# V of three batches by seven block products instead of eight, in an attention stage that shares its block sums

## The chip, the cores and the metric

The kernel runs on one core of a Trainium2 chip. Its time is the device time of one execution in microseconds. The core's engines are called PE (matrix products), ACT, DVE and POOL (elementwise work) and SP (which issues most DMAs); each works through its own queue in order, and they wait for each other through semaphores.

## What is computed

A decoder layer on x of 4 batches, 1024 tokens, 512 features, all in float32: self-attention, a gated convolution with a second input and a feed-forward product, each followed by a residual addition and a normalisation. The change touches only the attention's projections:

```python
q = _lin(_lin(x, wq_w, wq_b), vq_w, vq_b)      # k and v likewise
q = q.reshape(b, s, hc, H).transpose(2, 0, 1, 3)   # 32 heads of width 16
scores = jnp.einsum('cbqh,cbkh->cbqk', q, k) / scale
attn = jax.nn.softmax(scores, axis=-1)
o = jnp.einsum('cbqk,cbkh->cbqh', attn, v)
```

The two linear maps of each projection are folded into one 512x512 matrix (w_q, w_k, w_v) at the start.

## The kernel before

**Units and steps.** The attention works on 32 units, u = 0 to 31: batch b = u // 8 and a group g = u % 8 of four heads. A unit has 32 steps, h = 0 to 31, in an order written out by hand (the loop from line 754). Each step issues two things on PE: `nat` (L568), raw scores of unit u+1, of which DVE takes the row maxima (`mx`, L584), and `scores` (`st`, L638) of unit u, of which ACT takes the exponential (`at`, L649). After every second step comes one slot of other PE work: at h % 4 == 1 a weighing (`av`, L664: the weights times V, then a copy on ACT, L675, or an addition on DVE, L677), at h % 4 == 3 one piece of the list `fill`. At steps 15 and 31 DVE joins the maxima of half a unit (`neg`, L590) and transposes them, and SP moves them into the rows of q.

**What fills the slots.** In units 0 to 23 a unit's eight slots hold six pieces of the q or k projection of later units and two pieces of V of the next batch. All of these use `by_quarters` (L59), whose four matmuls of 32 columns of weights each go to the four quarters of PE. A V piece (`project_v`, L531 to 542) is 16 matmuls of 256 columns: 128 tokens by half the features, over all four 128-rows of the input. DVE adds the bias while it writes the piece from PSUM into `v_sb` (L536), whose rows have 17 words per head. Units 24 to 31 hold no V.

**q and k by seven products.** From unit 4 on, q and k use Strassen-Winograd block products: the 512 x 1024 x^T is cut into 2x2 blocks (b11, b21, b12, b22), two neighbouring 128-column blocks of the weights are cut into a11 to a22, and `product` (L451 to 493) computes one of the seven products in parts of 256 or 512 columns, 8 matmuls each. ACT copies each part out of PSUM (L477, L479), into its place in a pack or into one of two `rooms`; POOL adds the parts together (L482 to L493). `sum_x` (L428) makes four sums of x^T's blocks with POOL once per batch, in 1024 columns each, and `sum_w` (L442) four sums of the weights' blocks. `to_quadrants` (L392) moves a finished pack to the units' q and k with DMAs.

**PSUM.** `st`, `av` and the pieces of `fill` share `ps_st`, four banks in rotation; `nat` has two tiles of two banks each.

**The end of a unit.** `normalise` (L683) runs in four stages at steps 5, 9, 13 and 20 of the next unit: SP fetches the denominators, DVE inverts them, SP spreads them by DMA over the tile `rbc` (L703; two tiles, used in turn), POOL multiplies (`o_n`, L711) and SP stores the result. At step 5 of unit 24, loads for the later stages begin, and POOL adds a bias to the loaded residual `y` (L100).

Of the kernel before, what the change touches and what calls it, by code (L numbers as in the profile page):

```python
# [8 lines left out]
F32 = mybir.dt.float32  # L9
AF = mybir.ActivationFunctionType  # L10
ALU = mybir.AluOpType
# [3 lines left out]
P = 128  # L15
B, S, D = 4, 1024, 512
NH, HD = 32, 16
# [3 lines left out]
VW = HD + 1  # L21
# [230 lines left out]
def attention(ctx, tc, a, attn_d, ident, shared, hand):  # L252
    nc = tc.nc
# [4 lines left out]
    w_v = shared.tile([P, FT, D], F32, tag="w_v", name="w_v")  # L258
# [7 lines left out]
    def load_x(b):  # L266
# [2 lines left out]
            nc.sync.dma_start(t[:, f, :], a["xT"][b, f * P : (f + 1) * P, :])  # L269
        return t  # L270


    once = ctx.enter_context(tc.tile_pool(name="aonce", bufs=1))


    v_sb = []
# [7 lines left out]
    nc.vector.tensor_reduce(  # L284
        ones_row, ident.rearrange("p (j r) -> p r j", j=4)[:, HD, :], AX.X, ALU.add
    )
    q_ts, k_ts, rbcs = [], [], []
    for n, pool in ((3, shared), (1, once)):
        t = pool.tile([P, 8 if n == 3 else 2, S], F32, tag=f"qk{n}", name=f"qk{n}")
        for i in range(n):  # L290
# [8 lines left out]
    extra = shared.tile([P, 4, FT, TR], F32, tag="xf", name="extra").rearrange("p e t m -> p (e t m)")  # L299
    packs.append(extra[:, 0 : 2 * S].rearrange("p (n s) -> p n s", n=2))  # L300
    rooms = [extra[:, n : n + 256] for n in (2 * S, 2 * S + 256)]
    x_sums = []
    for n in range(2):
        t = shared.tile([P, 4, D + 1], F32, tag="u", bufs=2, name=f"x_sums{n}")
        x_sums += [t[:, 0:2, 0:512], t[:, 2:4, 0:512]]
    w_sums = shared.tile([P, FT, D], F32, tag="w_f", name="w_sums")
    w_sums = w_sums.rearrange("p (n i) (k o) -> p n (i k) o", n=2, o=P).rearrange("p n (i k) o -> p n i k o", i=4)

# [4 lines left out]
        negs.append(t)  # L313

    rbcp = ctx.enter_context(tc.tile_pool(name="arbc", bufs=1))
    for i in range(2):
        t = rbcp.tile([P, S], F32, tag=f"rbc{i}", name=f"rbc{i}")
        nc.gpsimd.memset(t, 0.0)
        rbcs.append(t)

    small = ctx.enter_context(tc.tile_pool(name="asmall", bufs=2))
    dpool = ctx.enter_context(tc.tile_pool(name="rec_d", bufs=2, space=bass.MemoryType.DRAM))
# [6 lines left out]
    xts = {}  # L329
# [54 lines left out]
                nc.vector.tensor_copy(w_d[:, f, :], pts[f])  # L384
    units = [(b, g) for b in range(B) for g in range(NG)]
    NU = len(units)
    QW = 256
    HS = 32


# [34 lines left out]

    def sum_x(b):  # L428
        b11, b21, b12, b22 = (
            xts[b][:, 2 * k : 2 * k + 2, 512 * t : 512 * t + 512] for t in range(2) for k in range(2)  # L430
        )
        t1, t2, t3, t4 = x_sums
        for dst, one, two in ((t1, b12, b11), (t2, b22, t1), (t3, b22, b12), (t4, t2, b21)):
            nc.gpsimd.tensor_tensor(dst, one, two, ALU.subtract)

    def blocks_of_w(p, which):
        w = (w_q, w_k)[which]
        return [
            w[:, 2 * k : 2 * k + 2, gg * P : (gg + 1) * P] for gg in (p % 4, p % 4 + 1) for k in range(2)
        ]  # L440

    def sum_w(p, which):  # L442
        a11, a12, a21, a22 = blocks_of_w(p, which)
        s1, s2, s3, s4 = (w_sums[:, which, i, :, :] for i in range(4))
        tt = nc.gpsimd.tensor_tensor
        tt(s1, a21, a22, ALU.add)
        tt(s2, s1, a11, ALU.subtract)
        tt(s3, a11, a21, ALU.subtract)
        tt(s4, a12, s2, ALU.subtract)

    def product(p, which, i, t0, n):  # L451

        b, gg = divmod(p, 4)
        a11, a12, _, a22 = blocks_of_w(p, which)
        s1, s2, s3, s4 = (w_sums[:, which, k, :, :] for k in range(4))
        t1, t2, t3, t4 = x_sums
        b11, b21, _, b22 = (
            xts[b][:, 2 * k : 2 * k + 2, 512 * t : 512 * t + 512] for t in range(2) for k in range(2)
        )
        left, right = {  # L460
            1: (a11, b11), 2: (a12, b21), 3: (s4, b22), 4: (a22, t4), 5: (s1, t1), 6: (s2, t2), 7: (s3, t3)
        }[i]
        cols = slice(t0, t0 + n)
        pt = ps_st.tile([P, 512], F32, tag="st", name=f"part{i}_{p}_{which}_{t0}")[:, 0:n]
        by_quarters(nc, pt, lambda k: left[:, k, :], lambda k: right[:, k, cols], 2)
        c11, c12, c21, c22 = (
            packs[which][:, o, 512 * t + t0 : 512 * t + t0 + n] for o in range(2) for t in range(2)
        )
        if i in (2, 3, 4):
            dst = rooms[0]  # L470
            rooms.reverse()
            dst = dst[:, 0:n]
        else:
            dst = {1: c11, 5: c22, 6: c12, 7: c21}[i]
        if i in (1, 7):
            bias = (b_q, b_k)[which][:, gg : gg + 1] if i == 1 else b_diff[:, which, gg // 2 : gg // 2 + 1]
            nc.scalar.activation(dst, pt, AF.Identity, bias=bias, scale=1.0)  # L477
        else:
            nc.scalar.copy(dst, pt)  # L479
        add = nc.gpsimd.tensor_add  # L480
        if i == 6:
            add(c12, c12, c11)  # L482
        elif i == 2:
            add(c11, c11, dst)
        elif i == 7:
            add(c21, c21, c12)
        elif i == 5:
            add(c12, c12, c22)
            add(c22, c22, c21)
        elif i == 3:  # L490
            add(c12, c12, dst)
        elif i == 4:
            nc.gpsimd.tensor_sub(c21, c21, dst)  # L493
# [37 lines left out]
    def project_v(b, t, half):  # L531

        pt = ps_st.tile([P, QW], F32, tag="st", name=f"v{b}_{t}_{half}")
        cols = slice(half * QW, half * QW + QW)
        by_quarters(nc, pt, lambda f: xts[b][:, f, t * P : (t + 1) * P], lambda f: w_v[:, f, cols])
        nc.vector.tensor_add(  # L536
            v_sb[b % 2][:, t, 16 * half * VW : 16 * (half + 1) * VW].rearrange("p (c h) -> p c h", h=VW)[
                :, :, 0:HD
            ],
            pt.rearrange("p (c h) -> p c h", h=HD),  # L540
            b_v[:, cols].rearrange("p (c h) -> p c h", h=HD),
        )

    def v_pieces(b, t):
        return [lambda half=half: project_v(b, t, half) for half in range(2)]

    def out_piece(b, t, c0, c1):
        pt = ps_st.tile([P, QW], F32, tag="st", name=f"po{b}_{t}_{c0}")
# [133 lines left out]

    def normalise(u, stage):  # L683
        b, g = units[u]
        o_sb, rbc = o_sbs[u], rbcs[u % 2]
        if stage == 0:

            den = small.tile([P, 32], F32, tag="den", name=f"den{u}")
            for j in range(4):
                nc.sync.dma_start(  # L690
                    den[32 * j : 32 * j + 32, :],
                    o_sb[32 * j + HD : 32 * j + HD + 1, :].rearrange("p (q r) -> p q r", r=32),
                )
            recs[u] = den
        elif stage == 1:
            rec = small.tile([P, 32], F32, tag="rec", name=f"rec{u}")
            nc.vector.reciprocal(rec, recs[u])
            rec_d = dpool.tile([4, S], F32, tag="rec_d", name=f"rec_d{u}")
            nc.sync.dma_start(rec_d.rearrange("j (q r) -> (j q) r", r=32), rec)
            recs[u] = rec_d  # L700
        elif stage == 2:
            for j in range(4):
                nc.sync.dma_start(  # L703
                    rbc[32 * j : 32 * j + HD, :], recs[u][j, :].partition_broadcast(HD)
                )
        else:
            o_n = onp.tile([P, 2, 512], F32, tag="o_n", name=f"o_n{u}")
            for half in range(2):
                cols = slice(512 * half, 512 * half + 512)

                nc.gpsimd.tensor_mul(  # L711
                    o_n[:, :, half * 256 : half * 256 + 256],
                    o_sb[:, cols].rearrange("p (s e) -> p e s", e=2),
                    rbc[:, cols].rearrange("p (s e) -> p e s", e=2),
                )

            for j in range(4):
                c = 4 * g + j
                for e in range(2):
                    r = c // 2 * 32 + e * HD  # L720
                    nc.sync.dma_start(
                        attn_d[c % 2 * 2 + b // 2][r : r + HD, b % 2 * 512 : b % 2 * 512 + 512],
                        o_n[32 * j : 32 * j + HD, e, :],
                    )
# [20 lines left out]
        nc.vector.tensor_tensor(b_diff[:, which, :], bias[:, 1::2], bias[:, 0::2], ALU.subtract)  # L745
    for piece in early[2:] + qk_pieces(0, 1) + folds[:5]:
        piece()
    sum_x(0)
    sum_w(2, 0)
    sum_w(2, 1)  # L750
    nc.sync.dma_start(b_d.rearrange("(t p) -> p t", p=P), b_vc)
# [2 lines left out]
    for u in range(-1, NU):  # L754
# [13 lines left out]
        if u == -1:  # L768
            fill = folds[5:] + qk_pieces(1, 0) + qk_pieces(1, 1) + [
                piece for t in range(NT) for piece in v_pieces(0, t)  # L770
            ] + fill
        elif units[u][0] + 1 < B:
            vs = v_pieces(units[u][0] + 1, units[u][1])
            fill = fill + vs if w == 3 else vs + fill
        if w == 2 and p + 2 < NU // 2:
            due.setdefault((u, 24), []).append(lambda p=p: sum_w(p + 2, 0))
        if w == 0 and u >= 0 and p < NU // 2:
            due.setdefault((u, 24), []).append(lambda p=p: sum_w(p, 1))
        if w == 3 and p % 4 == 2 and p // 4 + 1 < B:
            due.setdefault((u, 28), []).append(lambda p=p: sum_x(p // 4 + 1))  # L780
        if u == -1:
            xts[1] = load_x(1)
        elif units[u][1] == 5 and units[u][0] + 2 < B:
# [37 lines left out]
        else:  # L821
# [38 lines left out]
                    hand.load_residual(2)  # L860
            assert not fill
        if u == -1:
            setup.close()
            atp = ctx.enter_context(tc.tile_pool(name="at", bufs=14))
            obuf = ctx.enter_context(tc.tile_pool(name="obuf", bufs=2))
            onp = ctx.enter_context(tc.tile_pool(name="onp", bufs=1))
# [332 lines left out]
```

## Time and profile before

| what | value |
|---|---|
| median of 3 runs | 2428.03 us (2427.80 to 2428.67) |
| the profiled execution | 2427.53 us |
| its span, first to last instruction | 2425.7 us |
| PE busy | 2410.5 us |
| DVE busy | 1747.9 us |
| ACT busy | 1329.0 us |
| POOL busy | 588.5 us |
| mean granted clock of PE | 0.999 |

The profile lists, for groups of instructions, the line, the engine, the operation, the tiles written and read, the count, the busy time, the mean time of one in ns, and the idle time before them with what ended it. Its timeline gives start, duration, engine, line and tiles of single instructions or runs of them, all from the start of the span; a bracket names the idle time before and the instruction that ended it. PEld is the loading of weights into PE, which overlaps its matmuls; each float32 matmul leaves two records. The chain is the work that ended last, followed back from the end. The stage of units 0 to 23 lies between about 149 and 1464 us.

### The profile page before, as it was taken

What the parts mean: (1) busy time and instruction counts of PE and PEld (TensorE: products, weight loads), DVE (VectorE), ACT (ScalarE), POOL (GpSimd) and SP (SyncE); (2) the same over time, 40 slices, a digit from 0 to 9 for tenths busy, and PEclk for the clock granted to TensorE, in tenths of its full rate; (3) what the DMA queues carried; (4) which work ended last, traced back from release to release, by engine and by line L of the source; (5) the groups of instructions that cost most, each with busy time, mean ns of one, the idle gap of its engine ahead of it and who ended that gap; (6) DMA issues with size and microseconds to landing.
All of it is one profiled execution on the core that took longest, in us unless ns stands there. A gap on an engine that the chain in (4) does not pass through costs nothing.

```text
span 2425.7 us, 70210 instructions
## 1 busy us (share of the span) xinstructions
PE 2410.5 (99%) x30380; PEld 1626.6 (67%) x30380; DVE 1747.9 (72%) x2197; ACT 1329.0 (55%) x2593; POOL 588.5 (24%) x537
## 2 busy tenths in 40 slices
PE   9999999999999999999999999999999999999998
PEld 5556666666666666666666666566666799747994
DVE  3577777777777777777777777677777477878677
ACT  1056666666666666666666666566666723411333
POOL 5011311111122212111311201311210267422661
PEclk9999999999999999999999999999999999999999
DMA  6200112011001111111110012102200242160311
GB/s 222 59 3 17 28 23 56 17 30 26 17 17 30 21 54 22 25 21 20 27 25 17 17 34 93 41 17 48 89 17 12 81 149 87 70 226 18 122 35 70
DMA packets 80838, 121.45 MB, mean 50 GB/s; under 512 B 39072, under 2 KB 39328, under 8 KB 80528
## 3 DMA queue, kind: packets, MB, share of 16 engines
q1 hardware_dynamic: 79808, 115.77, 16.8%
q8 instruction: 239, 3.92, 0.7%
q10 hardware_dynamic: 720, 1.18, 0.1%
q14 instruction: 71, 0.58, 0.1%
HBM read 80.77 MB, written 18.35 MB: 41 GB/s over the span
## 4 chain that ended last, share of the span: by engine, by line
PE 97%; DVE 1%; POOL 0%; ACT 0%; DMA 0%; issue 0%; SPq 0%; DVEq 0%; POOLq 0%; ACTq 0%
PE nat L568 22%; PE av L664 20%; PE st L638 18%; PE part L59 8%; PE pc L948 6%; PE pa L948 6%; PE v L59 5%; PE pf L1032 4%; PE po L59 2%; PE po L241 2%; PE proj L59 1%; PE fold L377 1%; PE fold L59 1%; PE tr L1024 0%; PE nats L568 0%; POOL y L100 0%
## 5 line engine op out<-in xcount | busy, mean ns | idle before, releaser
L584 DVE TENSOR_REDUCE mx<-nat 128x2 f32<-128x1024 f32 x1008 | 1188.0, 1220 | 402.8 <-PE st L638 375.0
L649 ACT ACTIVATE at<-st 128x512 f32<-128x512 f32 x2016 | 1043.2, 603 | 541.6 <-PE st L638 529.8
L568 PE MATMUL nat<-qk 32*128 32x512 f32 x4032 | 1011.8, 614 | 0.5 <-DVE mx L584 0.5
L638 PE MATMUL st<-qk 32*128 32x256 f32 x8064 | 1002.0, 387 | 3.7 <-ACT extra L479 3.7
L638 PEld LDWEIGHTS st<-qk 32*128 32x128 f32 x8064 | 685.7, 184 | 48.8 <-ACT extra L479 4.5
L664 PE MATMUL av<-at,v_sb 128*32 128x256 f32 x8192 | 499.6, 383 | 1.4 <-ACT at L649 1.4
L568 PEld LDWEIGHTS nat<-qk 32*128 32x128 f32 x4032 | 344.0, 184 | 220.1 <-DVE mx L584 136.6
L664 PEld LDWEIGHTS av<-at,v_sb 128*32 128x32 f32 x8192 | 241.7, 110 | 223.1 <-ACT at L649 90.2
L948 PE MATMUL pc<-xf,w 128*128 128x171 f32 x1024 | 159.9, 308 | 0.6 <-DVE o_sb L677 0.6
L948 PE MATMUL pa<-xf,w 128*128 128x171 f32 x1024 | 159.8, 308 | 0.0
L948 PEld LDWEIGHTS pc<-xf,w 128*128 128x128 f32 x1024 | 152.0, 189 | 1.7 <-DVE o_sb L677 1.1
L948 PEld LDWEIGHTS pa<-xf,w 128*128 128x128 f32 x1024 | 152.1, 189 | 0.0
L711 POOL TENSOR_TENSOR o_n<-o_sb,rbc 128x512 f32<-128x512 f32 x64 | 97.7, 1547 | 170.9 <-DMA rbc<-rec_d 132.8
L959 ACT ACTIVATE u<-u,b_c 128x512 f32<-128x512 f32 x64 | 46.2, 721 | 161.1 <-DVE u L958 161.1
L59 PE MATMUL v<-w_v,xT 128*32 128x256 f32 x2048 | 121.7, 382 | 0.0
L1032 PE MATMUL pf<-w_f,xq_t 128*128 128x512 f32 (+1 forms) x264 | 115.2, 581 | 1.7 <-ACT xq_t L1026 1.5
L677 DVE TENSOR_TENSOR o_sb<-av,o_sb 128x256 f32<-128x256 f32 x128 | 54.4, 425 | 73.6 <-PE av L664 73.1
L170 POOL TENSOR_TENSOR w<-w 128x512 f32<-128x512 f32 x64 | 81.8, 1311 | 92.9 <-DMA w<-in_conv_wT 61.1
L482 POOL TENSOR_TENSOR qk<-qk 128x256 f32<-128x256 f32 x14 | 10.1, 724 | 380.1 <-ACT qk L479 379.9
L59 PEld LDWEIGHTS v<-w_v,xT 128*32 128x32 f32 x2048 | 61.1, 109 | 55.0 <-ACT at L649 16.5
L675 ACT COPY o_sb<-av 128x256 f32<-128x256 f32 x128 | 48.0, 375 | 78.0 <-PE av L664 63.4
L59 PE MATMUL part<-x_sums,w_sums 128*32 128x256 f32 (+1 forms) x896 | 83.6, 490 | 0.0
(139 smaller groups left out, 1810.4 us busy)
## 6 DMA issues: line engine op xcount, KB each, us to landing
w<-in_conv_wT SPq DMA_DIRECT2D x32, 512.0 KB
u<-in_ctx SPq DMA_DIRECT2D x16, 1024.0 KB
xT<-in_xT SPq DMA_DIRECT2D x16, 512.0 KB
qk<-qk SPq DMA_DIRECT2D x128, 64.0 KB
qk<-extra SPq DMA_DIRECT2D x128, 64.0 KB
rbc<-rec_d SPq DMA_DIRECT2D x128, 64.0 KB
attn<-o_n SPq DMA_DIRECT2D x256, 32.0 KB
big<-attn SPq DMA_DIRECT2D x4, 2048.0 KB
```

The source lines that it names most:

```text
L59: nc.tensor.matmul(pt[r, :], lhsT(f)[:, r], rhs(f), start=f == 0, stop=f == tiles - 1)
L170: self.nc.gpsimd.tensor_tensor(w[:, i, tap, :], w[:, i, 0, :], w[:, i, 1, :], op)
L241: nc.tensor.matmul(pt, attn_t[:, f, t * P : (t + 1) * P], self.w_o[:, f, cols], start=f == 0, stop=f == FT - 1)
L568: nc.tensor.matmul(pts[n], q_ts[u % 4][r : r + 32, qt * P : (qt + 1) * P], k_ts[u % 4][r : r + 32, kh * 512 : kh * 512 + 512], start=True, ...
L584: nc.vector.tensor_reduce(mxs[u][:, qt, 2 * pair : 2 * pair + 2, kh], pt, AX.X, ALU.max, negate=True)
L638: nc.tensor.matmul(st[:, k * QW : k * QW + QW], k_ts[u % 4][r : r + 32, kt * P : (kt + 1) * P], q_ts[u % 4][r : r + 32, qq * QW : qq * QW ...
L649: nc.scalar.activation(at, st, AF.Exp, scale=0.25)
L664: nc.tensor.matmul(av[32 * j : 32 * j + 32, :], v_sb[b % 2][:, kt, c * VW : c * VW + 32], ats[u, 2 * i + n // 2, j][:, n % 2 * QW : n % 2 ...
L677: nc.vector.tensor_add(o, av, o)
L711: nc.gpsimd.tensor_mul(o_n[:, :, half * 256 : half * 256 + 256], o_sb[:, cols].rearrange("p (s e) -> p e s", e=2), rbc[:, cols].rearrange( ...
L948: nc.tensor.matmul(pt, w[:, i, tap, o : o + P], xf[:, tap, i, :], start=i == 0, stop=i == FT - 1)
L1032: nc.tensor.matmul(pt, xq_ts[b, t][:, f, :], hand.w_f[:, f, cols], start=f == 0, stop=f == FT - 1)
```

## The change

- **V of batches 1 to 3** is computed by the same seven block products. Two 256-column halves of w_v and two 256-row halves of its input make the weights' blocks; POOL forms their four sums once, at step 8 of unit 0. Tokens t and t + 4 (in tiles of 128) are the two token blocks, so a product for one t is 128 tokens by 256 columns over half the input: 8 matmuls. There are 28 of them per batch: 12 PSUM tiles take two, 4 tiles take one. ACT copies each product into a room, and POOL adds it to one, two or three places of `v_sb`, for product 1 with the bias: 52 additions of 256 columns per batch. Batch 0 keeps `project_v`.
- **x^T's sums** are shared by q, k and V. The third (b22 - b12) is written in place of b12, and the four subtractions are spread over steps 26, 28, 30 and 0 instead of standing together at step 28. The freed quarter of `x_sums` and a new tile hold w_v's sums.
- **Rooms**: four instead of two until unit 24 (the new pair is the tile of `b_o`, which is loaded in unit 24).
- **One `rbc` tile** instead of two.
- **Order**: in units with u % 4 == 1 or 3 (w = 0 and 2) the V pieces stand third and sixth of the eight slots instead of first and second; the other units keep their order.

```diff
-    for i in range(2):
-        t = rbcp.tile([P, S], F32, tag=f"rbc{i}", name=f"rbc{i}")
-        nc.gpsimd.memset(t, 0.0)
-        rbcs.append(t)
+    rbc = rbcp.tile([P, S], F32, tag="rbc", name="rbc")
+    nc.gpsimd.memset(rbc, 0.0)
...
+    t = shared.tile([P, D], F32, tag="b_o", name="rooms")
+    rooms += [t[:, 0:256], t[:, 256:512]]
...
+    def sums_of_x(b):
+        b11, b21, b12, b22 = blocks_of_x(b)
+        t1, t2, t4 = x_sums
+        sub = nc.gpsimd.tensor_sub
+        return [
+            lambda: sub(t1, b12, b11),
+            lambda: sub(t2, b22, t1),
+            lambda: sub(t4, t2, b21),
+            lambda: sub(b12, b22, b12),
+        ]
...
+    def v_products(b, parts):
+        pt = ps_st.tile([P, 512], F32, tag="st", name=f"v{b}_" + "_".join(f"{i}{t}" for i, t in parts))
+        made = []
+        for n, (i, t) in enumerate(parts):
+            left, right = operands(i, v_blocks, v_sums, b)
+            part = pt[:, n * QW : n * QW + QW]
+            by_quarters(nc, part, lambda k: right[:, k, t * P : t * P + P], lambda k: left[:, k, :], 2)
+            made.append(part)
...
+        kept = []
+        for part in made:
+            kept.append(room())
+            nc.scalar.copy(kept[-1], part)
...
+            if i == 1:
+                add(c12, x, b1)
+                add(c21, x, b2)
+                add(c22, x, b2)
+            elif i == 2:
+                add(c11, c12, x)
+            elif i == 4:
+                nc.gpsimd.tensor_sub(c21, c21, x)
+            else:
+                for c in {3: (c12,), 5: (c12, c22), 6: (c12, c21, c22), 7: (c21, c22)}[i]:
+                    add(c, c, x)
+
+    v_parts = [[(1, t), (2, t)] for t in range(4)] + [[(3, 0), (3, 1)], [(3, 2), (3, 3)]]
+    v_parts += [[(6 - n, t), (7 - 3 * n, t)] for t in range(3) for n in range(2)]
+    v_parts += [[(i, 3)] for i in (6, 7, 5, 4)]
...
-            vs = v_pieces(units[u][0] + 1, units[u][1])
-            fill = fill + vs if w == 3 else vs + fill
+            b, g = units[u][0] + 1, units[u][1]
+            v1, v2 = (lambda n=n, b=b: v_products(b, v_parts[n]) for n in (2 * g, 2 * g + 1))
+            fill = {
+                0: fill[:2] + [v1] + fill[2:4] + [v2] + fill[4:],
+                1: [v1, v2] + fill,
+                2: fill[:2] + [v1] + fill[2:4] + [v2] + fill[4:],
+                3: fill + [v1, v2],
+            }[w]
...
-            due.setdefault((u, 28), []).append(lambda p=p: sum_x(p // 4 + 1))
+            for when, work in zip(((u, 26), (u, 28), (u, 30), (u + 1, 0)), sums_of_x(p // 4 + 1)):
+                due.setdefault(when, []).append(work)
+        if u == 0:
+            due.setdefault((0, 8), []).append(lambda: sum_blocks(v_blocks, v_sums))
+        if u == 24:
+            del rooms[:]
+            rooms.extend(extra[:, n : n + 256] for n in (2 * S, 2 * S + 256))
```

More of the change, by code (lines that the diff above doesn't have):

```diff
@@ L270, in load_x @@
         return t
+    QW = 256
     once = ctx.enter_context(tc.tile_pool(name="aonce", bufs=1))
@@ L286, in attention @@
     )
-    q_ts, k_ts, rbcs = [], [], []
+    q_ts, k_ts = [], []
     for n, pool in ((3, shared), (1, once)):
@@ L305, in attention @@
         x_sums += [t[:, 0:2, 0:512], t[:, 2:4, 0:512]]
+    t = x_sums.pop()
+    v_sums = [t[:, i, :].rearrange("p (k o) -> p k o", k=2) for i in range(2)]
+    t = once.tile([P, 2, 2, QW], F32, tag="v_sums", name="v_sums")
+    v_sums += [t[:, i, :, :] for i in range(2)]
     w_sums = shared.tile([P, FT, D], F32, tag="w_f", name="w_sums")
@@ L386, in attention @@
     NU = len(units)
-    QW = 256
     HS = 32
@@ L418, in qk_pieces, with blocks_of_x @@
         ]
[L428 to L434, printed above, removed]
+    def blocks_of_x(b):
+        return [xts[b][:, 2 * k : 2 * k + 2, 512 * t : 512 * t + 512] for t in range(2) for k in range(2)]
+    def sums_of_x(b):
[8 more added lines that the diff above has]
+        ]
     def blocks_of_w(p, which):
@@ L442, in sum_w, with sum_blocks @@
     def sum_w(p, which):
-        a11, a12, a21, a22 = blocks_of_w(p, which)
-        s1, s2, s3, s4 = (w_sums[:, which, i, :, :] for i in range(4))
+        sum_blocks(blocks_of_w(p, which), [w_sums[:, which, i, :, :] for i in range(4)])
+    def sum_blocks(blocks, sums):
+        a11, a12, a21, a22 = blocks
+        s1, s2, s3, s4 = sums
         tt = nc.gpsimd.tensor_tensor
@@ L449, in sum_w, with operands, room @@
         tt(s4, a12, s2, ALU.subtract)
+    def operands(i, blocks, sums, b):
+        a11, a12, _, a22 = blocks
+        s1, s2, s3, s4 = sums
+        t1, t2, t4 = x_sums
+        b11, b21, t3, b22 = blocks_of_x(b)
+        return {
+            1: (a11, b11), 2: (a12, b21), 3: (s4, b22), 4: (a22, t4), 5: (s1, t1), 6: (s2, t2), 7: (s3, t3)
+        }[i]
+    def room():
+        rooms.append(rooms.pop(0))
+        return rooms[-1]
     def product(p, which, i, t0, n):
         b, gg = divmod(p, 4)
[L454 to L462, printed above, removed]
+        left, right = operands(i, blocks_of_w(p, which), [w_sums[:, which, k, :, :] for k in range(4)], b)
         cols = slice(t0, t0 + n)
@@ L469, in product @@
         if i in (2, 3, 4):
-            dst = rooms[0]
-            rooms.reverse()
-            dst = dst[:, 0:n]
+            dst = room()[:, 0:n]
         else:
@@ L545, in v_pieces @@
         return [lambda half=half: project_v(b, t, half) for half in range(2)]
+    v_blocks = [w_v[:, 2 * k : 2 * k + 2, QW * o : QW * o + QW] for o in range(2) for k in range(2)]
+    def v_products(b, parts):
[6 more added lines that the diff above has]
+            made.append(part)
+        heads = lambda x, w: x.rearrange("p (c h) -> p c h", h=w)[:, :, 0:HD]
+        b1, b2 = (heads(b_v[:, o * QW : o * QW + QW], HD) for o in range(2))
+        kept = []
+        for part in made:
+            kept.append(room())
+            nc.scalar.copy(kept[-1], part)
+        add = nc.gpsimd.tensor_add
+        for (i, t), x in zip(parts, kept):
+            c11, c12, c21, c22 = (
+                heads(v_sb[b % 2][:, tt, 16 * o * VW : 16 * (o + 1) * VW], VW) for o in range(2) for tt in (t, t + 4)
+            )
+            x = heads(x, HD)
+            if i == 1:
[12 more added lines that the diff above has]
+    v_parts += [[(i, 3)] for i in (6, 7, 5, 4)]
     def out_piece(b, t, c0, c1):
@@ L684, in normalise @@
         b, g = units[u]
-        o_sb, rbc = o_sbs[u], rbcs[u % 2]
+        o_sb = o_sbs[u]
         if stage == 0:
@@ L747, in attention @@
         piece()
-    sum_x(0)
+    late_sum = sums_of_x(0)
+    for work in late_sum[:3]:
+        work()
     sum_w(2, 0)
@@ L862, in attention @@
         if u == -1:
+            late_sum[3]()
             setup.close()
```

## The prediction

> **What bounds the kernel now.** I read the page first: its busy shares, its slices, the chain that ended last.
>
> ```profile
> PE 2410.5 (99%) x30380; PEld 1626.6 (67%) x30380; DVE 1747.9 (72%) x2197; ACT 1329.0 (55%) x2593; POOL 588.5 (24%) x537
> ...
> PE 97%; DVE 1%; POOL 0%; ACT 0%; DMA 0%; issue 0%; SPq 0%; DVEq 0%; POOLq 0%; ACTq 0%
> PE nat L568 22%; PE av L664 20%; PE st L638 18%; PE part L59 8%; PE pc L948 6%; PE pa L948 6%; PE v L59 5%; PE pf L1032 4%; PE po L59 2%; PE po L241 2%; PE proj L59 1%; PE fold L377 1%; PE fold L59 1%; PE tr L1024 0%; PE nats L568 0%; POOL y L100 0%
> ```
>
> PE is 97% of the chain and the V products (v, L59) are 5% of it. In the table by stages PE is busy 451.00 of 451 us from 149 to 600 us, and as fully up to 1464 us, while POOL is busy 79.10 of those 451. So in units 0 to 23, where all of the change lies, only PE's own work counts, until some other engine makes PE wait. The waits of PE agree: in the whole run one wait for an evacuation is above 2 us (PE st <- ACT extra L479, 3.7 us, once, in unit 24).
>
> Next, what a product costs **in its place**. PE runs a strict beat: two steps of scores and maxima (1.93 us), then one slot, filled in turn by a weighing (av) and by a projection. The timeline of PE, first around a V slot, then around a slot with half as many matmuls:
>
> ```profile
> 290.69 1.93 PE L59 MATMUL v<-w_v,xT 128*32 128x256 f32 x32
> 292.56 0.70 PE L568 MATMUL nat<-qk 32*128 32x512 f32 x2
> ```
>
> ```profile
> 560.87 1.07 PE L59 MATMUL part<-x_sums,w_sums 128*32 128x256 f32 x16
> ...
> 561.87 0.19 PEld L568 LDWEIGHTS nat<-qk 32*128 32x128 f32 x2 [0.41 <-issue]
> 561.87 0.70 PE L568 MATMUL nat<-qk 32*128 32x512 f32 x2
> ```
>
> The next work starts 1.87 us after the 32-record slot and 1.00 us after the 16-record one (a matmul leaves two records). The beat after either is the same, so half a slot is worth 0.87 us on the path.
>
> The Trainium skill (Perfetto Trace Analysis, Identifying the Most-Contended Engine) warns that matmul busy time says little about PE and asks for the weight loads' share. That is 67% here, and read by it alone a third of PE would be free and the saving could be near 0. The two slots above speak against it for this stretch: the time follows the matmuls.
>
> **The change, part by part.**
>
> V's matmuls. Before, 16 V slots per batch of 16 matmuls each. After, 28 products (7 by 4 token tiles) of 8 matmuls: 12 slots with two products and 4 with one. The built order of PE shows the same: 12 full slots and 4 half ones per batch, in the same number of places, so the slot count and the beat stay. Saved: 3 batches x 4 half slots x 0.87 = **10.4 us**. (By busy time: 3/32 of v's 121.7 us = 11.4; I take the beat, since busy time counts the overlapping ends.) A full slot with two products is priced as a full slot of before: the same 16 matmuls of the same shape.
>
> Emptying the V bank. Before, DVE did it in one addition; now ACT copies, once per product, and both copies of a full slot wait for the slot's end. The slot above again, with what follows:
>
> ```profile
> 292.69 0.43 DVE L536 TENSOR_TENSOR v_sb<-v,b_v 128x256 f32<-128x256 f32 x1 [0.40 <-PE v L59]
> ...
> 293.74 0.60 PE L638 MATMUL st<-qk 32*128 32x256 f32 x4
> 293.81 1.09 ACT L649 ACTIVATE at<-st 128x512 f32<-128x512 f32 x2 [1.73 <-PE st L638]
> ```
>
> ps_st has four banks and each beat takes five tiles, so the V bank is wanted again by the fourth score tile after it, at 293.74. ACT is idle from the end of its exponentials (about 292.07) to 293.81. Two copies from 292.69 at 0.405 us each (ACT copy L479, 128x256) end at 293.50, 0.24 us before the bank is wanted; at 0.499 each (the slower L477 form) at 293.69, still before. So 84 copies (34 us of ACT) cost nothing, hidden behind the next beat's matmuls; with that cover gone, each 0.1 us of lateness costs 36 full slots x 0.1 = 3.6 us. DVE loses 48 additions of 0.425 us (20 us), worth nothing on the path: a reduction there waits for PE st, not for the addition.
>
> POOL. It gains 52 additions per batch, 156 in all, of 256 columns whose output rows are 17 words apart. No such row exists. Bounds: 0.72 us (L482, 256 contiguous columns) and 1.55 us (L711, 512 columns with a stride); I take 0.75, nearest to the row of the same size: 117 us over 24 units. The heaviest slot has 5 additions, 3.8 us (7.8 at the upper end), and slots are about 7 us apart. What waits for POOL is the next use of a room, four allocations later with four rooms, so two slots or more; the move to units; and the weighing of the next batch. Cost nothing at 0.75. The four sums of w_v (4 x 1.27, unit 0) and the split sums of x^T (the same four subtractions of 2.0 to 2.5 us) lie in POOL's idle time too; x^T's fourth, in place, is needed at step 11 of the next unit and is queued by its step 0.
>
> A collision with DVE. Twice a unit DVE joins the maxima (neg, L590, two SBUF inputs), usually in 0.19 us; where POOL started at the same moment it stretched:
>
> ```profile
> 1487.79 0.45 POOL L484 TENSOR_TENSOR qk<-qk,extra 128x128 f32<-128x128 f32 x1 [5.91 <-ACT extra L479]
> 1487.80 0.48 DVE L590 TENSOR_TENSOR neg<-mx 128x16 f32<-128x16 f32 x1
> ```
>
> That beat took 2.34 us from 1486.74 to 1489.08 instead of 1.93, so one collision costs PE 0.4 us. L590 comes about 7.3 us after the end of the slot before; five additions at 0.75, begun 0.6 us after it, are done at 4.4. They reach L590 only from about 1.35 us each. Then at most 9 or so places are hit (6 slots of five additions, 3 spots beside x^T's sums): 3.6 us. I take 0.3 us, for x^T's sums alone, which end some 0.4 us before L590.
>
> The Trainium skill (SBUF — State Buffer, Who interferes with whom) has this rule: a DVE instruction with two SBUF inputs and a GpSimd one that reads SBUF block each other for whole instructions, which speaks against moving V to POOL. By the rule with nothing known of the spacing, 48 L590 at the measured 0.4 us would be an estimated 19 us and eat the gain; the spacing above is why I don't take it.
>
> One denominator tile. Its next write must wait for POOL's last reading. o_n of a unit ends at 566.20 (563.21 + 2.99), the next rbc DMA is issued at 603.59; in the tightest unit 1759.18 against 1797.03, at the end of attention 1922.26 against 1945.35. No wait ends late, SP keeps its order: nothing either way. The second tile's memset (0.95 us of POOL at the start) goes, while PE is busy folding weights: nothing.
>
> Extra waits. A slot whose first matmul waits for two engines starts about 0.06 us later (beats of 1.99 instead of 1.93 us before the first uses of w_sums); some 6 V slots gain one: 0.4 us.
>
> Unit 24's wait of 3.7 us (POOL stands behind the loading of y, ACT behind POOL's rooms). There are two rooms again from unit 24, so it should stay; if y lands a little sooner against the beat it goes: 0 to -3.7, taken at 0.
>
> **Sum**: -10.4 + 0.3 + 0.4 = -9.7. The profiled execution took 2427.53 us (span 2425.7 and 1.8 around it): 2417.8. The median of the runs is 0.5 above it, so I say **2418 us**.
>
> **Rivals.**
> 1. Unit 24's wait goes as well: 2418 - 3.7 = 2414. For it: it hangs on one DMA's landing. Against it: nothing in that unit is changed.
> 2. The half slots don't pay, because DVE or ACT then sets the beat: 2427 to 2428. For it: DVE works 2.36 us of a pair of steps. Against it: beats with 16-record slots already run at 2.93 us with reductions waiting 0.58 us for PE.
> 3. Slower: the V bank is handed back late. In each of 36 full slots the fourth score tile would wait for ACT's second copy, or for a room that POOL still holds. At 9.7 / 36 = 0.27 us per slot the gain is gone, from (9.7 + 4.9) / 36 = 0.41 us the kernel is slower by over 0.2%, at 0.6 it takes 2418 + 21.6 = 2440. For it: the cover is only 0.24 us, and POOL's new shape is unmeasured. Against it: even the slower ACT form fits, and POOL would need over 5 us for an addition (28 us from a pair of rooms' filling to their next, less some 3 us of other work, over five additions) to keep a room that long.
> 4. The change not doing what it says: excluded, the order holds 96 matmuls fewer.
>
> **How the numbers follow.** About 0.2% (4.9 us) is what a measurement of this kernel can tell from no change. Forecast, with its bounds (-11.4 to -6.4): 0.74. Rival 1: 0.10. Rival 2, with partial losses by L590 or late banks that leave under 4.9 us: 0.10. Rival 3: 0.06. Faster 0.84, same 0.10, slower 0.06. Range: from rival 1's 2414 to 2423, which is the upper bound of POOL's additions (+3.6) and 0.04 us of lateness at each full slot (+1.4) on top of 2418.
>
> **What would show it.** Right: v's busy time near 110 us, 12 half V slots of 1.00 us, full ones still 1.87, beats after them 1.93, ACT copies of V done before the fourth score tile, POOL additions at 0.72 to 1 us, busy POOL near 710 us. Wrong: PE st or av waiting for an ACT copy of V, L590 rows above 0.3 us in units 0 to 23, ACT waiting for POOL at a room, or rbc DMAs that wait for o_n.

## The result and the profile after

| what | before | after |
|---|---|---|
| median of 6 runs each | 2426.50 us (2424.51 to 2428.67) | 2416.14 us (2414.51 to 2419.02) |
| ratio, 95% interval | 1 | 0.9957 [0.9946, 0.9967] |
| the profiled execution | 2427.53 us | 2419.02 us |
| stretch from the first beat after 149 us to the end of unit 23's work | 1338.48 us | 1328.13 us |
| of it, 379 beats (two steps each) | 736.23 us | 736.16 us |
| POOL busy | 588.5 us | 695.1 us |

The kernel became 10.4 us (0.43%) faster, by more than the 0.2% that can be told apart. Three runs of before were added to the three known at the time of the prediction; they brought its median from 2428.03 to 2426.50. The stretch runs from 152.46 to 1490.94 us in before and from 152.82 to 1480.96 in after. (Units 0 to 23 themselves run from 130.7 to 1486.7 us in before; the 149 and 1464 given further up cut off both ends.) It holds all of the change but the first two V slots, which are full, and w_v's sums. It is shorter by 10.35 us, and the beats in it are in sum as long as before. The gain is in the slots.

The page of after, its busy shares and its chain. Line numbers are higher than before: `nat` is now L630, `st` L700, `av` L726, `neg` L652.

```profile
PE 2401.5 (99%) x30188; PEld 1621.4 (67%) x30188; DVE 1727.4 (71%) x2149; ACT 1356.2 (56%) x2677; POOL 695.1 (29%) x696
...
PE 97%; DMA 1%; POOL 1%; DVE 0%; ACT 0%; issue 0%; DVEq 0%; POOLq 0%; ACTq 0%
PE nat L630 21%; PE av L726 20%; PE st L700 19%; PE part L59 8%; PE pc L1026 6%; PE pa L1026 6%; PE v L59 4%; PE pf L1110 4%; PE po L59 3%; PE po L241 2%; PE proj L59 1%; PE fold L383 1%; DMA y<-in_x 1%; PE tr L1102 1%; PE fold L59 1%; PE nats L630 0%
```

PE has 192 records fewer (96 matmuls) and its share of the chain is still 97%; v has gone from 5% to 4% of it. New in the chain are 1% each for POOL and for `DMA y<-in_x`: that is unit 24, treated below.

A full V slot in the timeline of after, the one that stood at 290.69 before:

```profile
290.87 1.93 PE L59 MATMUL v<-v_sums,xT 128*32 128x256 f32 x32
...
292.74 0.70 PE L630 MATMUL nat<-qk 32*128 32x512 f32 x2
...
292.92 0.65 ACT L585 COPY extra<-v 128x256 f32<-128x256 f32 x2 [0.72 <-PE v L59]
...
293.37 1.33 POOL L602 TENSOR_TENSOR v_sb<-v_sb,extra 128x256 f32<-128x256 f32 x2 [4.45 <-ACT extra L585]
...
293.61 0.27 PEld L700 LDWEIGHTS st<-qk 32*128 32x128 f32 x2
...
293.91 0.59 PE L700 MATMUL st<-qk 32*128 32x256 f32 x3
```

The slot still takes 1.87 us. The two ACT copies end 0.84 us after it (293.57 against 292.73) where DVE's one addition ended at 0.56. The row of score matmuls at 1.18 (293.91), which the prediction took for the start of the fourth score tile, is still in its place. But the timeline joins single records into rows, and by the records this tile's first matmul is earlier, at 0.97 in both kernels; the row at 1.18 holds later records of the third and fourth tile. The fourth tile's **weight load** comes at 0.88 (0.62 in before), just after the copies' end; that detail matters below.

A half slot of after, with one product:

```profile
1442.43 1.07 PE L59 MATMUL v<-x_sums,x_sums 128*32 128x256 f32 x16
1443.44 0.70 PE L630 MATMUL nat<-qk 32*128 32x512 f32 x2
```

The next work starts 1.00 us after it. By all start times of the two traces, 48 V slots of 1.864 us (mean) became 36 of 1.866 and 12 of 1.003.

POOL's new additions, two of their groups of after (count, busy us, mean ns of one, idle time before them and what ended it):

```profile
L602 POOL TENSOR_TENSOR v_sb<-v_sb,rooms 128x256 f32<-128x256 f32 x48 | 31.5, 687 | 155.3 <-ACT rooms L585 155.3
...
L595 POOL TENSOR_TENSOR v_sb<-rooms,b_v 128x256 f32<-128x256 f32 x6 | 4.4, 737 | 0.0
```

0.69 to 0.74 us each, a little under the 0.75 taken.

### The profile page after: what moved, and what is told of

Same layout as the page of the kernel before. It is cut to its first block, busy times and chain, and to the rows that moved or that the text cites. A ratio compares the mean times of both kernels' runs of the same rounds, so it can differ in the third digit from the quotient of the medians.

```text
span 2417.2 us, 70121 instructions
## 1 busy us (share of the span) xinstructions
PE 2401.5 (99%) x30188; PEld 1621.4 (67%) x30188; DVE 1727.4 (71%) x2149; ACT 1356.2 (56%) x2677; POOL 695.1 (29%) x696
## 3 DMA queue, kind: packets, MB, share of 16 engines
q10 hardware_dynamic: 720, 1.18, 0.1%
## 4 chain that ended last, share of the span: by engine, by line
PE 97%; DMA 1%; POOL 1%; DVE 0%; ACT 0%; issue 0%; DVEq 0%; POOLq 0%; ACTq 0%
PE nat L630 21%; PE av L726 20%; PE st L700 19%; PE part L59 8%; PE pc L1026 6%; PE pa L1026 6%; PE v L59 4%; PE pf L1110 4%; PE po L59 3%; PE po L241 2%; PE proj L59 1%; PE fold L383 1%; DMA y<-in_x 1%; PE tr L1102 1%; PE fold L59 1%; PE nats L630 0%
## 5 line engine op out<-in xcount | busy, mean ns | idle before, releaser
L630 PE MATMUL nat<-qk 32*128 32x512 f32 x4032 | 1012.7, 614 | 0.5 <-DVE mx L646 0.5
L700 PE MATMUL st<-qk 32*128 32x256 f32 x8064 | 1004.3, 388 | 4.1 <-ACT extra L499 4.1
L700 PEld LDWEIGHTS st<-qk 32*128 32x128 f32 x8064 | 692.6, 184 | 48.4 <-ACT extra L499 5.0
L726 PE MATMUL av<-at,v_sb 128*32 128x256 f32 x8192 | 499.7, 383 | 1.4 <-ACT at L711 1.4
L630 PEld LDWEIGHTS nat<-qk 32*128 32x128 f32 x4032 | 344.4, 184 | 221.1 <-DVE mx L646 132.9
L726 PEld LDWEIGHTS av<-at,v_sb 128*32 128x32 f32 x8192 | 241.7, 110 | 223.0 <-ACT at L711 90.0
L1110 PEld LDWEIGHTS pf<-w_f,xq_t 128*128 128x128 f32 x264 | 47.9, 190 | 48.3 <-issue 45.4
L602 POOL TENSOR_TENSOR v_sb<-v_sb,rooms 128x256 f32<-128x256 f32 x48 | 31.5, 687 | 155.3 <-ACT rooms L585 155.3
L1033 DVE SCALAR_TENSOR_TENSOR u<-pa,u 128x342 f32<-128x342 f32 x64 | 40.6, 634 | 49.6 <-PE pa L1026 46.9
L117 ACT ACTIVATE rstd<-mv,eps 128x2 f32<-128x2 f32 (+3 forms) x32 | 9.5, 297 | 111.5 <-DVE mv L107 61.6
```

What stands on the lines that cost most here:

```text
L630: nc.tensor.matmul(pts[n], q_ts[u % 4][r : r + 32, qt * P : (qt + 1) * P], k_ts[u % 4][r : r + 32, kh * 512 : kh * 512 + 512], start=True, ...
L700: nc.tensor.matmul(st[:, k * QW : k * QW + QW], k_ts[u % 4][r : r + 32, kt * P : (kt + 1) * P], q_ts[u % 4][r : r + 32, qq * QW : qq * QW ...
L726: nc.tensor.matmul(av[32 * j : 32 * j + 32, :], v_sb[b % 2][:, kt, c * VW : c * VW + 32], ats[u, 2 * i + n // 2, j][:, n % 2 * QW : n % 2 ...
L1110: nc.tensor.matmul(pt, xq_ts[b, t][:, f, :], hand.w_f[:, f, cols], start=f == 0, stop=f == FT - 1)
```

## The experiments

Five questions: where the gain is, what unit 24 costs, how much room the V bank's emptying had, what POOL's work could have cost, and whether the other edits matter. Each group of runs has its own runs of before beside it: medians of 2426.05, 2426.03 and 2426.99 us, in the order below.

### 1. The half slots filled up again

The theory: the gain is 96 matmuls. The rival: it comes from DVE's lighter load or the new order, and the half slots pay little. The changed kernel again, and one in which each half slot computes its product a second time into the other half of its bank, so that PE has all its matmuls back and everything else stays:

```diff
             made.append(part)
+        if len(parts) == 1:
+            by_quarters(nc, pt[:, QW : 2 * QW], lambda k: right[:, k, t * P : t * P + P], lambda k: left[:, k, :], 2)
```

> The changed kernel once more, as the base for the others of this group. Theory (12 half slots of PE, 0.863 us each): 0.9957 of before, -10.4 us. Its profile should show the same beat (36 full V slots of 1.865, 12 of 1.003 us), and a wait in unit 24 that may differ by a microsecond or two from run to run.

> The four lone products of each batch are computed twice into the same bank, so that PE does 16 matmuls in all 16 V slots; nothing else is changed, the second half is not read. Theory (the gain is the 96 matmuls): 12 x 0.863 = +10.4 us over the changed kernel, 0.999 to 1.001 of before. Rival (the gain comes from DVE's relief, the new order or the rooms): stays at 0.9957, half the gain or more is kept.

Measured: the changed kernel 2416.01 us (0.9953 [0.994, 0.9965]); with full half slots 2427.36 (1.0003 [0.9994, 1.0012]). The whole gain is gone. Over the same 700 pieces of PE's order up to the first 128-column slot of unit 23 the two differ by 10.3 us (1237.9 against 1227.6). The rival falls: DVE keeps its 48 fewer additions and POOL its 156 more, and neither is worth anything on the path.

### 2. Unit 24: y's additions moved

In both kernels one stand-still of PE remains. Its timeline in after:

```profile
1511.15 9.18 POOL L100 TENSOR_TENSOR y<-y,b_o 128x512 f32<-128x512 f32 x8 [26.18 <-DMA y<-in_x]
...
1524.97 0.37 ACT L499 COPY extra<-part 128x256 f32<-128x256 f32 x1 [5.33 <-POOL qk L511]
...
1525.40 1.80 PE L700 MATMUL st<-qk 32*128 32x256 f32 x6 [4.14 <-ACT extra L499]
...
1527.13 3.64 PE L726 MATMUL av<-at,v_sb 128*32 128x256 f32 x32
```

Read upwards from the third line: PE's scores wait 4.14 us for ACT's copy out of a PSUM bank; that copy waits 5.33 us for POOL to free its room; POOL had been held for 9.18 us by eight additions to y in a row, which began when the transfer of y had landed. Then look at the weighing: 3.64 us instead of 1.93, with no wait in it. The table by stages (PE, PEld, DVE, ACT, POOL busy, granted clock, DMA share, GB/s) is cut where the granted clock changes. First of after, then of before, then of the kernel of experiment 1 with full half slots, whose PE waited 2.50 us at this place:

```profile
1522.30:1525.70 3.40, 0.30 (x2) 0.30 (x4) 0.49 (x1) 0.73 (x2) 3.32 (x5) 1.00 0.00 0
1525.70:1529.10 3.40, 3.40 (x26) 1.66 (x26) 0.00 (x0) 1.83 (x4) 3.40 (x3) 0.50 0.02 5
1529.10:1532.50 3.40, 3.40 (x28) 1.93 (x24) 0.42 (x1) 0.00 (x0) 0.14 (x1) 0.50 0.26 65
1532.50:1535.90 3.40, 3.40 (x50) 2.30 (x47) 2.57 (x3) 2.46 (x6) 0.65 (x1) 1.00 0.04 12
```

```profile
1532.80:1536.20 3.40, 1.17 (x10) 0.78 (x14) 0.05 (x1) 1.59 (x4) 3.40 (x4) 1.00 0.00 0
1536.20:1539.60 3.40, 3.40 (x32) 1.34 (x30) 0.00 (x0) 0.75 (x2) 2.67 (x3) 0.50 0.07 17
1539.60:1543.00 3.40, 3.40 (x50) 2.35 (x50) 2.64 (x3) 2.14 (x5) 0.00 (x0) 1.00 0.25 63
```

```profile
1528.40:1531.80 3.40, 2.15 (x22) 1.12 (x18) 2.82 (x3) 0.53 (x2) 3.24 (x3) 1.00 0.01 2
1531.80:1535.20 3.40, 2.15 (x26) 1.35 (x30) 0.28 (x1) 2.34 (x5) 3.40 (x5) 1.00 0.00 0
```

After the stand PE runs at a granted clock of 0.50, for 6.8 us in after and for 3.4 us in before, and then at 1.00 again. So the stand costs more than its wait. The edit moves the eight additions of units 24 and 28 out of the tight place, to single steps later in the unit:

```diff
-        if b % 2 == 0:
-            for t in range(NT):
-                nc.gpsimd.tensor_add(self.y[b][:, t, :], self.y[b][:, t, :], self.b_o)
+    def add_b_o(self, b, t):
+        self.nc.gpsimd.tensor_add(self.y[b][:, t, :], self.y[b][:, t, :], self.b_o)
...
+        if u in (24, 28):
+            b = u // 2 - 12
+            for t, when in enumerate(((u, 22), (u, 23), (u, 26), (u, 27), (u, 30), (u, 31), (u + 1, 2), (u + 1, 3))):
+                due.setdefault(when, []).append(lambda b=b, t=t: hand.add_b_o(b, t))
```

> The eight additions of the bias to y on POOL are put at steps 22 to 31 and 2, 3, behind the landing of y, instead of right after the load in units 24 and 28. Theory (PE stands in unit 24 because POOL waits for y and then ACT for a room, and the clock is low after the stand): the unit's long beat of 7.9 us, its slow weighing of 3.6 us and the beat after it go, -8.5 us against the changed kernel, and the 0.85 us of unit 28 too: 2407 to 2409 where the changed kernel takes 2416 to 2417. Rival (only the 4.1 us of standing counts): -4 to -5 us. Rival (the stand moves elsewhere): no gain.

The same edit in the kernel before:

> The same move in the kernel before. Theory: its stand of unit 24 costs 6.5 us (beat 6.77 instead of 1.93, weighing 3.52 instead of 1.86), unit 28 0.85: -7.3 us, 0.997 of before. With it in both kernels their difference is the half slots alone, 10.4 us.

Measured: 2409.52 us (0.9928 [0.9915, 0.994]) with the change and 2419.90 (0.9972 [0.9961, 0.9983]) without it. The edit is worth 6.5 and 6.2 us, somewhat less than the 8.5 and 7.3 expected from two traces in which PE stood for long. Some 0.7 us of what the traces gain lies in unit 28, where both kernels had a beat of 2.78 us that is 2.09 us with the edit. The change is worth 10.4 us between the two, as between the kernels with the stand. No wait of PE for an ACT copy is left in its trace. This is the **best version** of the study, ahead of both kernels. It also steadies the time: runs spread over 1.9 us, against 4.5 in after.

How long PE stands differs from run to run: the changed kernel's two traces have 3.23 and 4.14 us. From four traces with the stand (the beat is 1.93 us without it, the weighing 1.86 from start to next start):

| kernel | PE waits | beat | weighing | next beat |
|---|---|---|---|---|
| half slots filled | 2.50 us | 5.56 us | 1.86 us | 1.93 us |
| changed, again | 3.23 | 6.97 | 3.57 | 2.81 |
| before | 3.71 | 6.77 | 3.52 | 1.93 |
| after | 4.14 | 7.88 | 3.57 | 2.81 |

After 2.50 us of waiting the clock held; after 3.23 it halved. The length of the wait is not the whole of it. In the four traces the clock changes at steps of one length: it stays at one value for 3.41, 6.83, 880.6 or 884.1 us, which is 1, 2, 258 and 259 times 3.413. It fell at the end of steps in which PE was busy for 0.30 us (after), 0.34 (changed, again) and 1.17 (before) of 3.40; the wait of 2.50 us fell across two steps with 2.15 each, and the clock held. The Trainium skill (TensorE: Matmul & The Clock Gate, Part 1: The HAM clock gate) says that an idle window of about 3.4 us takes the clock to half, and that the window runs freely. The steps of 3.41 us agree with it; that the window must be idle throughout does not, since PE was busy for a third of the one in before. Why the half clock lasts one step in before and two in the others is not shown.

That also explains why the two profiled executions differ by only 8.5 us and not by 10.4: in after, the stand's beat (+1.11), the weighing (+0.05) and the next beat (+0.87) are 2.0 us longer than in before.

### 3. The V bank handed back later

The prediction gave ACT's two copies a cover of 0.24 us. On top of the best version, ACT copies the second product of a full slot once more, or twice more, into the same room. Expected by the theory: one more copy is nearly hidden; by the rival, it is not.

```diff
             nc.scalar.copy(kept[-1], part)
+        if len(parts) == 2:
+            for _ in range(1):
+                nc.scalar.copy(kept[-1], part)
```

> On top of y_late (2409.5 us): in each of the 36 full V slots ACT copies the second product twice into its room, so the bank is emptied one copy later. Theory: copies follow each other at 0.27 us, the third ends 1.10 us after the slot, the fourth score tile wants the bank at 1.18: no cost, beats after full V slots stay 1.93 us, 2409 to 2411. Rival (the prediction's cover of 0.24 us, counted with whole copies of 0.40): late by 0.15 us and more, 36 x 0.15 = +5 us.

> On top of y_late: three copies of the second product, so the bank is emptied two copies later. Theory: the last ends 1.37 us after the slot and the bank comes back 0.2 to 0.3 us late: beats after full V slots 2.1 to 2.3 us, 36 x 0.25 = +9 us, PE st waits for ACT rooms or extra. It would be the prediction's third rival made real. Rival (banks are not what bounds): no cost.

Measured: 2423.03 us (0.9989 [0.9979, 1.0]) and 2437.26 (1.0043 [1.0027, 1.0059]): 13.5 and 27.7 us over the best version. **The theory of the cover fell.** The second kernel is slower than before, so the third rival's mechanism is real. The timeline with one copy more, around a full slot that ended at 322.53:

```profile
322.53 0.70 PE L633 MATMUL nat<-qk 32*128 32x512 f32 x2
...
322.71 0.65 ACT L585 COPY extra<-v 128x256 f32<-128x256 f32 x2 [0.73 <-PE v L59]
...
323.39 0.37 ACT L588 COPY extra<-v 128x256 f32<-128x256 f32 x1
...
323.82 0.72 PEld L703 LDWEIGHTS st<-qk 32*128 32x128 f32 x6
...
324.14 0.81 PE L703 MATMUL st<-qk 32*128 32x256 f32 x4
...
324.88 1.93 PE L729 MATMUL av<-at,v_sb 128*32 128x256 f32 x32
```

The third copy ends at 323.76 and the fourth tile's load follows at 323.82. It is the load that waits for the bank: in the records it is the instruction with the wait, for ACT here and for DVE in before. The tile's first matmul is recorded together with the load, at 323.82; the row at 324.14 holds later ones. The same reading in four kernels, in us after the slot's end; the last column is the median beat after full V slots:

| kernel | last reader done | fourth tile's load | beat |
|---|---|---|---|
| before (one DVE addition) | 0.56 | 0.62 | 1.934 |
| after (two copies) | 0.84 | 0.89 | 1.947 |
| one copy more | 1.24 | 1.29 | 2.351 |
| two copies more | 1.65 | 1.70 | 2.755 |

From 0.84 on the beat grows with the reader's end, one for one (0.40 and 0.40). So the real deadline was at about 0.83, and the change's two copies already met it by 0.01 too late: 36 x 0.013 = 0.5 us in all. No cover was left.

A trap for readers of waits: the waits of PE's load side name the copies openly only where they are latest. With one copy more (13.5 us lost), then with two (columns: us in total, times, longest):

```profile
PEld st L703 <- ACT extra L588: 0.2, 1, 0.2
```

```profile
PEld st L703 <- ACT extra L588: 9.4, 18, 0.5
PEld st L703 <- ACT rooms L588: 9.1, 18, 0.5
```

0.2 of 13.5 us, then 18.5 of 27.7. The matmuls' own waits show neither. Idle time of the load side is counted from its previous load, and part of a late load shows nowhere but in the length of the beat. The beats should be measured, not only the waits.

### 4. POOL's additions multiplied

The rival: POOL's 156 additions collide with DVE's `neg` (two SBUF inputs), and each collision costs PE 0.4 us. On top of the best version each addition to V stands three or five times (adding and subtracting in turn, or writing the same sum again):

```diff
-        add = nc.gpsimd.tensor_add
+        def add(dst, one, two, ops=(ALU.add, ALU.subtract)):
+            for m in range(3):
+                nc.gpsimd.tensor_tensor(dst, one, two, ops[m % 2 if one is dst else 0])
...
-                nc.gpsimd.tensor_sub(c21, c21, x)
+                add(c21, c21, x, (ALU.subtract, ALU.add))
```

> On top of y_late: each addition into V is done three times on POOL (add, take away, add; or the same sum written again), so each costs 2.1 us in place of 0.69. Theory: no room is late; the only cost is the DVE instruction that joins the maxima, which POOL now meets in 12 to 18 of 48 places at 0.2 to 0.4 us each: +3 to +6 us, its duration over 0.3 us at these. Rival (POOL's time counts as such, 216 us more): +20 us and more. Rival (DVE is not held up): 0.

> On top of y_late: each addition five times, 3.45 us each, 430 us more of POOL in 1290 us. Theory: heaviest slot 17 us, rooms are used again 28 us later, so still no wait for a room; DVE is met at 24 to 36 places: +6 to +12 us. Rival (rooms bind already): ACT waits for POOL by microseconds and PE with it, +20 us and more.

Measured: 2409.41 us (0.993 [0.991, 0.9949]) and 2409.46 (0.9929 [0.991, 0.9949]), both the best version's time to 0.1 us, with POOL busy 908 and 1125 us. My expectation fell. The collisions were there. The group of `neg` in after, then with threefold additions:

```profile
L652 DVE TENSOR_TENSOR neg<-mx 128x16 f32<-128x16 f32 x64 | 13.4, 209 | 2.3
```

```profile
L655 DVE TENSOR_TENSOR neg<-mx 128x16 f32<-128x16 f32 x64 | 20.3, 318 | 2.3
```

The worst of them, in the timeline of the threefold kernel:

```profile
298.91 2.00 POOL L445 TENSOR_TENSOR x_sums<-x_sums,xT 128x1024 f32<-128x1024 f32 x1
299.04 1.91 DVE L655 TENSOR_TENSOR neg<-mx 128x16 f32<-128x16 f32 x1
299.28 0.70 PE L633 MATMUL nat<-qk 32*128 32x512 f32 x2
...
301.22 0.81 PEld L729 LDWEIGHTS av<-at,v_sb 128*32 128x32 f32 x20 [0.33 <-ACT at L714]
```

A 0.19 us instruction took 1.91 us: it started 0.13 after POOL's and ended 0.04 after it. The Trainium skill's rule (SBUF — State Buffer, Who interferes with whom) that the two block each other for whole instructions agrees with this row. But the beat that began at 299.28 was followed by a weighing at 301.22, 1.94 us later: PE did not notice. In the stretch 11 (threefold) and 22 (fivefold) `neg` were stretched. Compared beat by beat with the best version, none of the 350 beats up to unit 23's slot of 128 columns is longer by more than 0.015 us in either kernel.

That one is where my price of 0.4 came from. The beat from 1486.74 in before followed a slot of 128 columns (0.57 us). The other such slot, at 1492.88, has no collision near it and is followed by a beat of 2.28 us. The same two beats (2.34 and 2.28) stand in the traces of the best version and of the threefold and fivefold kernels. So nearly all of the length comes with the short slot ahead and not from the collision; the 0.05 us between the two beats stay open.

### 5. The other edits

On top of the best version: two rooms instead of four; V first in units u % 4 == 1 and 3, as before. On top of the kernel before with y's additions moved: one `rbc` tile.

```diff
-    rooms += [t[:, 0:256], t[:, 256:512]]
```

```diff
             fill = {
-                0: fill[:2] + [v1] + fill[2:4] + [v2] + fill[4:],
+                0: [v1, v2] + fill,
                 1: [v1, v2] + fill,
-                2: fill[:2] + [v1] + fill[2:4] + [v2] + fill[4:],
+                2: [v1, v2] + fill,
```

```diff
-    for i in range(2):
-        t = rbcp.tile([P, S], F32, tag=f"rbc{i}", name=f"rbc{i}")
-        nc.gpsimd.memset(t, 0.0)
-        rbcs.append(t)
+    t = rbcp.tile([P, S], F32, tag="rbc", name="rbc")
+    nc.gpsimd.memset(t, 0.0)
+    rbcs.append(t)
...
-        o_sb, rbc = o_sbs[u], rbcs[u % 2]
+        o_sb, rbc = o_sbs[u], rbcs[0]
```

> On top of y_late: two rooms instead of four throughout. Theory: rooms come free within one slot distance (about 7 us) while POOL's adds take at most 3.4 us, except where POOL has o_n (3 us), x^T's sums (2.2 us each) or w's sums (3 us) in its queue first; so ACT waits in some of the slots after those, and a wait at a full V slot holds a bank: 0 to +8 us. Rival (four rooms are needed for the gain): +10 us or more.

> On top of y_late: the V pieces of units with u % 4 of 1 or 3 stand first and second again. Theory: x^T's fourth sum ends at 304.64 in the changed kernel's profile and the first slot of unit 3 would start near 306.1, so no wait for POOL there; two heavy slots then follow each other (8 additions, 5.5 us, 7 us apart): within 0.1% of y_late. Rival (the order avoids a wait of PE on x^T's sums): three waits of 1 to 3 us, +3 to +9 us, seen as long beats in units 3, 11, 19.

> The kernel before with y's additions late and one tile of denominators instead of two, nothing else. Theory: the tile is free 23 us or more before its next write, no effect: within 0.1% of before_y_late (2419.9). Rival: SP waits for POOL's last product at the write and everything behind it in SP's queue is late: beats after steps 13 to 20 grow, +5 us or more.

Measured: two rooms 2409.56 us (0.9931 [0.9912, 0.9951]), the old order 2408.49 (0.9927 [0.9908, 0.9947]), one denominator tile 2419.59 (0.9972 [0.9962, 0.9983], against 2419.90 with two). None differs from its base by 0.05%, which is under what can be told apart. The two more rooms, the new places of V's pieces and the second denominator tile are each worth nothing measurable. If anything the new places cost a little: with the old order the 350 beats up to the slot of 128 columns are 0.6 us shorter in sum, and the time is 1.0 us lower. Two denominator tiles in the changed kernel were not tried.

## Why the prediction was right, and where only its sizes or reasons were not

**Half slots, -10.4.** Right in mechanism and size: 12 x (1.864 - 1.003) = 10.3 us, and the stretch is 10.35 shorter. Experiment 1 shows it by taking it away. The reading that carried it was to price a product by the start of the next work after a slot that existed already, not by busy time (11.4), nor by the loads' 67%, by which a third of PE would have been free.

**Emptying the V bank, 0, with a cover of 0.24 us.** The sum held by luck, since the reason did not. Two errors met. I let the fourth score tile ask for the bank at 1.18 after the slot. That was a misreading twice over: the row at 293.74 is not this tile's first matmul (0.97), and what asks for the bank is its load (from about 0.83). And I let the copies follow each other at 0.405 us (end at 0.94), when two copies into different rooms start 0.27 apart (end at 0.84). With the right deadline and my copies the term would have been about (0.94 - 0.83) x 36 = 4 us. The true term is +0.5; the cover is 0.

**POOL's additions, 0.** Right: 0.69 to 0.74 us each, and five times as many still cost nothing. Rooms held by POOL did not matter either, with two rooms instead of four.

**Collisions of `neg`, +0.3 (up to 3.6).** Mis-sized: 0. In after no `neg` of the stretch is stretched but the one that was so in before. The price of 0.4 us for one was a misreading of a beat that is long after a short slot with no collision too.

**Extra waits of V slots, +0.4.** Half of it is there: the beats ahead of four V slots (those at 290.87, 319.60, 768.45 and 1217.64) take 1.99 us, 0.06 more. The beats ahead of other slots got shorter by more: before's stretch has 35 beats of 1.99 us, after's has 14 and another 8 of 2.02. So 379 beats are 0.07 us shorter in sum than before, the 0.5 of the V bank included.

**One rbc tile, the memset, x^T's sums.** Nothing, as taken; the tile alone is shown by experiment 5, the other two were not run alone.

**Unit 24, 3.7 us that stay.** It stayed, so rival 1 did not come about. But it is not a fixed 3.7: with the halved clock behind it, moving y's additions is worth 6.2 to 6.5 us, and its length differs from run to run. It was taken from the waits alone, which show the wait and not the slow matmuls after it.

**Rivals 2 and 3.** The second would have needed DVE or ACT to set the beat; beats after half slots are as long as before. The third's place and mechanism were right, and it was nearer than stated: 0.40 us of ACT more per full slot, and the kernel is only 3 us ahead of before although unit 24 is mended, which alone is worth 6 us.

**The sum.** 2416.14 us against 2418: of the 1.9 us, 1.5 is the median of before, which went from 2428.03 to 2426.50 with more runs, and the rest the two small terms of +0.3 and +0.4, which the sum of the beats does not show, less the 0.5 of the bank. With unit 24's stand the runs of one kernel spread over 4 us, so an agreement closer than that is luck.

## What to carry to other kernels

Where one engine runs a strict beat, price work by the distance between starts around a unit of it that exists already, and test the price by putting the work back in. For a PSUM bank that is used in rotation, take the deadline from the weight load of the matmul that takes it next, and look at the length of the beat as well as at the waits. After a stand-still of PE, look at the granted clock behind it, since the loss can be twice the wait.

## What the hardware showed beyond that

- PE's granted clock changed at steps of 3.41 us. It fell to 0.50, for one step or two, after steps in which PE was busy for 0.30, 0.34 and 1.17 of 3.40 us, and not after steps with 2.15.
- The load of weights waits until the bank that its matmul will write has been read: it came about 0.05 us after the last reader's end in all four kernels, though in before nothing was late by it (load at 0.62, first matmul at 0.97). Where the bank came late, the first matmul is recorded together with its load.
- ACT copies of 256 columns out of PSUM take 0.37 us and start 0.27 apart when they write different rooms; the third, into the room just written, started 0.41 after the one before it. The Trainium skill (ScalarE: Activation LUTs, What ACT_TABLE_LOAD costs) has an overlap of about 93 ns between activations in a row; the first case agrees (0.37 - 0.27 = 0.10). In the second the copy carries a wait for a semaphore that ACT's own copies raise, and there is no overlap.
- A DVE instruction of 0.19 us took up to 1.91 us behind a POOL one and cost PE nothing.
